# Turning normalised rows: TensorE transposes, or VectorE blocks regrouped through device memory

## The chip, the cores and the metric

The kernel runs on one core of a Trainium2 chip. The metric is the device time of one execution in microseconds (us); a profiled execution also gives a trace, whose span runs from the first to the last instruction. The engines are named as in the profile: PE is TensorE (PEld its weight loads), DVE is VectorE, ACT is ScalarE, POOL is GpSimd, SP is SyncE, which issues nearly all DMA transfers here.

## The reference

The input x has 16 sequences of 256 tokens with 256 features, 4096 tokens in all, in float32. Two layers follow one another; each normalises, runs a mixer `s` and a gated network `g` on the normalised rows, and adds their product:

```python
xn = _layernorm(x, axis=-1)
s = _L0_attn_ref(xn, ...)          # linear recurrence over time, 32 complex states
g = _silu(_L0_ffn_ref(xn, ...))    # 256 -> 1024 (gelu) -> 256
x = x + s * g
xn = _layernorm(x, axis=-1)
s = _L1_attn_ref(xn, ...)          # causal attention, 16 heads, latent keys and values, rope
g = _silu(_L1_ffn_ref(xn, ...))    # base matrix plus routed low-rank part (top 2 of 8)
x = x + s * g
```

Every product with a weight matrix sums over the features. TensorE sums over partitions, so it needs the normalised rows with features on partitions, while the normalisation leaves tokens on partitions. Something has to turn each 128 x 128 block. How this is done is what changes here.

## The kernel before

The 4096 tokens are cut into 8 chunks of 512 (two sequences each). A chunk's rows `X[ch]` stay in SBUF as [128 tokens, 4 blocks, 256 features]. The normalised, turned chunk is `xnT`, [128 features, 2 halves, 512 tokens].

**Layer 0** is one loop over the chunks (from L454). Iteration `ch` does `hidden` (16 PE matmuls `ph`, for the chunk's two feature halves and eight blocks of the hidden layer, which the trace shows as 32 records of 512 columns, since it has two for each float32 matmul; then a gelu on ACT), `recur` (`pb`; then `v` on DVE, a swap of partition halves `w<-v` by two SP DMAs at L417 and L418, a POOL addition, a scan on DVE and a product that gives `g`), then for the next chunk `norm0` and `turn0`, and then two times `mix` (`pf`) and `finish0` (`py`, which reads `g`). PE's instructions are kept in the order of the program by the helper `InOrder` (L44 to L64); all of them therefore carry line L52 in the profile. The other engines' order in layer 0 is the framework's choice. `transpose_rows` (L156) makes eight PE transposes into PSUM (`tp`), and ACT and DVE copy one half each to `xnT`.

**Layer 1** keeps all five engines in program order. Before the loop, chunk 0 is prepared. The loop (L921) then runs over 64 units, one for each chunk, group of four heads and sequence: eight units per chunk, and `r` is the unit's place in its chunk. In the body of unit `i`:

- SP first fetches the turned probabilities of unit i-2 (`pT<-far`).
- `score_pack` runs three times (PE `sc`, DVE mask and maximum, ACT exponential), and POOL normalises.
- `turn` and `send` treat the probabilities of unit i-1: DVE transposes 32 x 32 blocks (`turned`), SP writes them to device memory in four DMAs (`far<-turned`), from where the fetch of the next unit reads them back in a regrouped order.
- In even units `query_move` issues eight DMAs (`qg<-qrot`), which put the rotated queries of the group that units i+2 and i+3 will use into place; and `values` multiplies the probabilities of units i-4 and i-3 with the values (PE `av`, reading `pT`).
- In odd units two, in even units one of the query products `pq` of a later group are made.
- The next chunk is prepared in between: `norm_begin` at r=0, `norm_end` at r=2, `transpose_chunk` at the end of r=2 (eight PE transposes, two ACT copies), `kv_begin` at r=4, `kv_end` at r=5, `router_chunk` at r=6, `key_chunk` at r=7. The output of the chunk before is finished (`po`) at r = 3, 4, 5 and 7.

Each engine works off its own list in order, so an instruction that waits holds back all behind it on its engine, also on SP's queue.

Of the kernel before, what the change touches and what calls it, by code (L numbers as in the profile page):

```python
# [11 lines left out]
F32 = mybir.dt.float32  # L12
# [6 lines left out]
P = 128  # L19
B, S, D = 16, 256, 256  # L20
NTOK = B * S
CH = 512
NCH = NTOK // CH
TPC = CH // P
# [16 lines left out]
def tile_two_layers(ctx: ExitStack, tc: tile.TileContext, d: dict, out: bass.AP):  # L41
    nc = tc.nc
# [96 lines left out]
    def layer_norm(pool, src, dst, tag):  # L139
# [10 lines left out]
        for j in range(TPC):  # L150
# [2 lines left out]
                ALU.subtract, ALU.mult,  # L153
            )

    def transpose_rows(psum, ptag, src, dst, tag):  # L156
        for c in range(2):
            ps = psum.tile([P, CH], F32, tag=ptag, name=f"tp_{tag}_{c}")
            for j in range(TPC):
                pe.transpose(  # L160
                    ps[:, j * P : (j + 1) * P], src[:, j, c * P : (c + 1) * P], ident
                )
            if c == 0:
                nc.scalar.copy(dst[:, c, :], ps)
            else:
                nc.vector.tensor_copy(dst[:, c, :], ps)

    def bc(ap, n):

        return ap.unsqueeze(1).to_broadcast([ap.shape[0], n, ap.shape[1]])  # L170
# [6 lines left out]
    with ExitStack() as l0:  # L177
# [3 lines left out]
        a2 = l0.enter_context(tc.tile_pool(name="a0", bufs=2))  # L181
        hpool = l0.enter_context(tc.tile_pool(name="h0", bufs=10))
        ps_mm = l0.enter_context(tc.tile_pool(name="ps_mm", bufs=4, space=PSUM))
# [4 lines left out]
        p1T = w0.tile([P, 2, FF], F32, tag="p1T", name="p1T")  # L188
# [27 lines left out]
        def norm0(ch):  # L216
            xn = a2.tile([P, TPC, D], F32, tag="xn", name=f"xn0_{ch}")
            layer_norm(sm, X[ch], xn, f"0_{ch}")
            return xn

        def turn0(ch, xn):
            xnT = a2.tile([P, 2, CH], F32, tag="xnT", name=f"xnT0_{ch}")
            transpose_rows(ps_mm, "mm", xn, xnT, f"0_{ch}")
            return xnT

        xn = norm0(0)
        xnT = turn0(0, xn)


# [23 lines left out]
        def tiny(name, n=1):  # L253
            return w0.tile([P, n], F32, tag=name, name=name)
# [38 lines left out]
        f = tiny("f")  # L293
# [12 lines left out]
        for k in range(1, 8):  # L306
            c, s = rot[:, k - 1, 0:1], rot[:, k - 1, 1:2]
# [10 lines left out]
        for k in range(8):  # L318
            n = 1 << k
            c, s = rot[:, k, 0:1], rot[:, k, 1:2]  # L320
# [17 lines left out]
        bT = w0.tile([P, 2, P], F32, tag="bT", name="bT")  # L338
# [52 lines left out]
        def hidden(ch, xnT):  # L391
            hT = []
            for fc in range(NFC):
                ph = ps_mm.tile([P, CH], F32, tag="mm", name=f"ph_{ch}_{fc}")
                for c in range(2):
                    pe.matmul(
                        ph, p1T[:, c, fc * P : (fc + 1) * P], xnT[:, c, :],
                        start=(c == 0), stop=(c == 1),
                    )
                ht = hpool.tile([P, CH], F32, tag="hT", name=f"hT_{ch}_{fc}")  # L400
                nc.scalar.activation(ht, ph, AF.Gelu, bias=b1[:, fc : fc + 1])  # L401
                hT.append(ht)
            return hT

        def recur(ch, xnT):

            pb = ps_mm.tile([P, 2, S], F32, tag="mm", name=f"pb_{ch}")
            for c in range(2):
                pe.matmul(
                    pb.rearrange("p b s -> p (b s)"), bT[:, c, :], xnT[:, c, :],  # L410
                    start=(c == 0), stop=(c == 1),
                )
            v = a2.tile([P, 2, S], F32, tag="v", name=f"v_{ch}")
            nc.vector.tensor_tensor(v, pb, bc(turn, 2), ALU.mult)

            w = a2.tile([P, 2, S], F32, tag="w", name=f"w_{ch}")
            nc.sync.dma_start(w[0:64, :, :], v[64:128, :, :])  # L417
            nc.sync.dma_start(w[64:128, :, :], v[0:64, :, :])  # L418
            nc.gpsimd.tensor_tensor(v, v, w, ALU.add)
            g = a2.tile([P, 2, S], F32, tag="g", name=f"g_{ch}")  # L420
            nc.vector.tensor_tensor_scan(
                g.rearrange("p b s -> p (b s)"), decay.rearrange("p b s -> p (b s)"),
                v.rearrange("p b s -> p (b s)"), 0.0, ALU.mult, ALU.add,
            )
            nc.vector.tensor_tensor(g, g, bc(turn, 2), ALU.mult)
            return g.rearrange("p b s -> p (b s)")
# [27 lines left out]
        for ch in range(NCH):  # L454
# [24 lines left out]
            xn, xnT = xn2, xnT2  # L479
# [3 lines left out]
    x1 = ctx.enter_context(tc.tile_pool(name="x1", bufs=2))  # L483
    qm = ctx.enter_context(tc.tile_pool(name="qm1", bufs=2))
    qr = ctx.enter_context(tc.tile_pool(name="qr1", bufs=1))
    a2 = ctx.enter_context(tc.tile_pool(name="a1", bufs=2))
    pp = ctx.enter_context(tc.tile_pool(name="p1", bufs=2))
    fix = ctx.enter_context(tc.tile_pool(name="fix1", bufs=1))
    qp = ctx.enter_context(tc.tile_pool(name="q1", bufs=2))
    dp = ctx.enter_context(tc.tile_pool(name="far1", bufs=3, space=bass.MemoryType.DRAM))  # L490

    sp = InOrder(nc.sync)
    ve = InOrder(nc.vector)
# [5 lines left out]
    def m1(name, shape):  # L499
        return ps_m1.tile(shape, F32, tag="m1", name=name)  # L500
# [4 lines left out]
    chunks = [Chunk() for _ in range(NCH)]  # L505
# [17 lines left out]

    def norm_end(ch):
        k = chunks[ch]
        k.xn = x1.tile([P, TPC, D], F32, tag="xn", name=f"xn1_{ch}", bufs=1)
        for j in range(TPC):
            ve.tensor_scalar(
                k.xn[:, j, :], X[ch][:, j, :], k.mv[:, j, 0:1], k.rs[:, j : j + 1],
                ALU.subtract, ALU.mult,  # L530
            )

    def transpose_chunk(ch):
        k = chunks[ch]
        k.xnT = x1.tile([P, 2, CH], F32, tag="xnT", name=f"xnT1_{ch}")
        for c in range(2):
            ps = m1(f"tp_1_{ch}_{c}", [P, CH])
            for j in range(TPC):
                pe.transpose(ps[:, j * P : (j + 1) * P], k.xn[:, j, c * P : (c + 1) * P], ident)
            ac.copy(k.xnT[:, c, :], ps)  # L540

    def kv_begin(ch):

# [275 lines left out]
    def send(u):  # L819

        u.far = dp.tile([4, 32, G, 3, P], F32, tag="far", name=f"far_{u.n}", bufs=3)
        for h in range(G):
            sp.dma_start(
                u.far[:, :, h, :, :].rearrange("k s z q -> s k z q"),
                u.turned[32 * h : 32 * h + 32, :, :, :],
            )
# [4 lines left out]
    def fetch(u):  # L831
        new_pT(u)
        sp.dma_start(u.pT, u.far.rearrange("k s h z q -> (k s) h z q"))
# [56 lines left out]

    norm_begin(0)
    norm_end(0)
    transpose_chunk(0)
    kv_begin(0)
    query_mm(0, 0)
    query_mul(0, 0)
# [24 lines left out]
    for i in range(LAST):  # L921
        ch, r = divmod(i, PER)
        odd = i % 2 == 1
        u, w = units[i], units[i - 1] if i else None
        here = w is not None and w.i >= LAST - 2
        n = (i + 3) // 2 if odd else (i + 2) // 2
        n = n if n < len(groups) else None
        more = ch + 1 < NCH
        last = ch - 1 if ch and r in FINISH else None

        if 2 <= i:
            fetch(units[i - 2])
        score_pack(u, 0)
        if w:
            normalise(w, (2,))
        if r == 1:
            gate_end(ch, 0)
        if r == 2:
            gate_end(ch, 1)
            if more:  # L940
                norm_end(ch + 1)
        if r == 5 and more:
            kv_end(ch + 1)
        if w:
            for z in (1, 2):
                turn_here(w, z) if here else turn(w, z)

        if r == 0:
            mid_chunk(ch)
        if r == 7 and more:  # L950
            key_chunk(ch + 1)
        if n is not None:
            query_mm(n, 0 if odd else 3)
            if not odd:
                query_lat(n, 3)
        score_pack(u, 1)

        if odd and n is not None:
            query_mm(n, 1)
            query_mul(n, 0)  # L960
        if w:
            if here:
                turn_here(w, 0)
            else:
                turn(w, 0)
                send(w)
        if not odd:
            if n is not None:
                query_move(n)
            if i >= 4:  # L970
                values(units[i - 4])
                values(units[i - 3])
        score_pack(u, 2)
        normalise(u, (0, 1))

        if odd and n is not None:
            query_mm(n, 2)
            query_mul(n, 1)
            query_rot(n)
            query_lat(n, 2)  # L980
        if r < 2:
            gate_begin(ch, r)
        if r == 0 and more:
            norm_begin(ch + 1)
        if r == 2 and more:
            transpose_chunk(ch + 1)
        if r == 4 and more:
            kv_begin(ch + 1)
        if r == 6 and more:
            router_chunk(ch + 1)  # L990
        if last is not None:
            j = FINISH.index(r)
            finish_mm(last, j, 0, NPAIR)
            finish_out(last, j)


    ch = NCH - 1
# [89 lines left out]
```

## Time and profile before

| | |
|---|---|
| median of 3 runs | 980.04 us (977.87 to 980.08) |
| profiled execution | 977.1 us, span 975.3 us |
| mean granted TensorE clock | 0.994 |
| PE busy | 935.6 us, 96% of the span |
| DVE, ACT, POOL busy | 60%, 44%, 44% |
| DMA packets, bytes | 197028, 136.04 MB |
| PE transposes `tp` | 128, median 273 ns each, overlapping |
| chunk of layer 0, chunk of layer 1 | 31.9 us, 82.0 us |

A timeline row gives the start and length in us, the engine, the source line, the operation, what it writes and reads, a shape and a count; in square brackets, where there is one, the idle time just before it on its engine and what ended it. The name of a tile is given without its buffer number. "SPq" rows are DMAs issued by SP, their length being the issue on SP and not the transfer; the tile view gives the time from issue to landing. A table of stretches gives for each engine the busy time and the number of instructions, then the granted TensorE clock, the mean busy share of the 16 DMA engines and GB/s.

### The profile page before, as it was taken

The numbers are of one execution on the slowest core, as the hardware profiler recorded it, in microseconds if no ns is written. First come the engines' busy times: TensorE is split into PE (matmuls) and PEld (weight loads), VectorE is DVE, ScalarE is ACT, GpSimd is POOL, SyncE is SP. The second block draws the span as 40 slices with busy tenths as digits, with TensorE's granted clock in tenths as the row PEclk, the third lists the DMA queues.
The fourth block names the chain that finished last, engine by engine and source line by source line (L and its number), as shares of the span: only waits on it lengthen the run. The fifth ranks groups of instructions, "written<-read, shape, count | busy, mean of one in ns | idle before, by whom it ended". The sixth has DMA issues, their size and how long they took to land.

```text
span 975.3 us, 15554 instructions
## 1 busy us (share of the span) xinstructions
PE 935.6 (96%) x4698; PEld 667.9 (68%) x4698; DVE 589.1 (60%) x1876; ACT 425.1 (44%) x1412; POOL 425.5 (44%) x749
## 2 busy tenths in 40 slices
PE   4999999999999989999999999999999999999986
PEld 2657657766666556777777777777777777777765
DVE  7923223221125968867876786786787679676651
ACT  2232232233324546544554454555456455455440
POOL 2316124213333545553655456456355544544542
PEclk9999999999999989999999999999999999999999
DMA  9622000000002577776767677678767776867850
GB/s 292 194 65 65 12 11 1 11 11 11 1 12 33 119 199 196 199 188 186 189 177 211 165 168 220 161 197 201 189 176 178 207 174 167 221 169 192 206 182 22
DMA packets 197028, 136.04 MB, mean 139 GB/s; under 512 B 142545, under 2 KB 186449, under 8 KB 196945
## 3 DMA queue, kind: packets, MB, share of 16 engines
q1 hardware_dynamic: 193712, 129.27, 50.9%
q0 software_dynamic: 1536, 4.20, 1.2%
q10 hardware_dynamic: 1696, 1.58, 0.7%
q8 instruction: 38, 0.62, 0.3%
q14 instruction: 46, 0.37, 0.1%
HBM read 63.18 MB, written 52.95 MB: 119 GB/s over the span
## 4 chain that ended last, share of the span: by engine, by line
PE 83%; DVE 6%; POOL 4%; DMA 3%; issue 2%; SPq 2%; ACT 0%; ACTq 0%; POOLq 0%; DVEq 0%
PE pq L52 20%; PE sc L52 13%; PE pf L52 10%; PE ph L52 10%; PE po L52 10%; PE av L52 8%; PE pg L52 4%; SPq L52 2%; PE pm L52 1%; POOL pr L52 1%; PE py L52 1%; PE pb L52 1%; PE pkv L52 1%; PE tp L52 1%; DVE nm L52 1%
## 5 line engine op out<-in xcount | busy, mean ns | idle before, releaser
L52 ACT ACTIVATE pr<-sc,nm 128x256 f32<-128x256 f32 (+7 forms) x512 | 189.5, 380 | 286.6 <-DVE sr L52 198.4
L52 POOL TENSOR_SCALAR pr<-pr,sr 128x256 f32<-128x256 f32 (+7 forms) x512 | 192.2, 394 | 275.6 <-DVE sr L52 272.6
L52 PEld LDWEIGHTS sc<-kT,qg 128*128 128x128 f32 x1024 | 159.7, 191 | 65.3 <-issue 39.5
L52 PE MATMUL sc<-kT,qg 128*128 128x256 f32 (+7 forms) x1024 | 176.6, 306 | 6.9 <-DMA qg<-qrot 4.2
L52 DVE STREAM_TRANSPOSE turned<-pr 128x512 f32<-128x512 f32 x186 | 123.2, 687 | 15.2 <-POOL pr L52 14.9
L52 DVE TENSOR_REDUCE nm<-sc 128x1 f32<-128x256 f32 (+7 forms) x512 | 127.6, 301 | 6.6
L52 PE MATMUL pq<-xnT,wlat 128*128 128x512 f32 x256 | 124.4, 609 | 0.0
L52 PE MATMUL pq<-xnT,wrope 128*128 128x512 f32 x256 | 120.1, 593 | 0.0
L52 PE MATMUL po<-wout,attT 128*128 128x256 f32 x512 | 115.8, 380 | 0.0
L52 PE MATMUL pf<-p2T,hT 128*128 128x256 f32 x512 | 113.0, 379 | 0.0
L52 PE MATMUL ph<-xnT,p1T 128*128 128x512 f32 x256 | 112.9, 600 | 0.0
L52 PEld LDWEIGHTS po<-wout,attT 128*128 128x128 f32 x512 | 96.4, 190 | 20.9 <-issue 6.6
L52 PEld LDWEIGHTS pf<-p2T,hT 128*128 128x128 f32 x512 | 96.7, 190 | 13.3 <-issue 0.5
L52 ACT ACTIVATION_READ_ACCUMULATOR pr<-sc,nm 128x1 f32 x512 | 103.5, 202 | 0.0
L52 PE MATMUL av<-pT,row 128*64 128x256 f32 (+1 forms) x1024 | 90.5, 329 | 0.3 <-DMA pT<-far 0.3
L52 PEld LDWEIGHTS ph<-xnT,p1T 128*128 128x128 f32 x256 | 49.1, 192 | 59.3 <-issue 57.9
L52 POOL TENSOR_TENSOR qrot<-qmul,qmul 128x512 f32<-128x512 f32 x64 | 83.0, 1318 | 14.6 <-DVE sc L52 9.9
L52 DVE TENSOR_TENSOR qmul<-pq,rot_q 128x512 f32<-128x512 f32 x128 | 80.7, 672 | 0.0
L52 PEld LDWEIGHTS av<-pT,row 128*64 128x64 f32 x1024 | 64.2, 137 | 23.1 <-PE av L52 0.5
L52 ACT ACTIVATE qg<-pq 64x512 f32<-64x512 f32 x128 | 75.4, 589 | 6.7 <-PE pq L52 6.0
L52 DVE TENSOR_TENSOR sc<-sc,kmask 128x96 f32<-128x96 f32 (+1 forms) x192 | 45.8, 238 | 51.1 <-PE sc L52 49.8
L401 ACT ACTIVATE hT<-ph,b 128x512 f32<-128x512 f32 x64 | 44.0, 687 | 59.0 <-PE ph L52 58.9
(178 smaller groups left out, 906.1 us busy)
## 6 DMA issues: line engine op xcount, KB each, us to landing
far<-turned SPq DMA_DIRECT2D x248, 192.0 KB, 3.7
pT<-far SPq DMA_DIRECT2D x62, 768.0 KB, 4.6
qg<-qrot SPq DMA_DIRECT2D x256, 64.0 KB, 2.4
out_dram<-o POOLq DMA_DIRECT2D x32, 128.0 KB, 2.9
x<-in_x_dram SPq DMA_DIRECT2D x7, 512.0 KB, 8.7
wqn<-in_wq_nopeT_dram SPq DMA_DIRECT2D x4, 512.0 KB, 4.7
wo<-in_Wo_dram SPq DMA_DIRECT2D x4, 512.0 KB, 5.3
w<-v SPq DMA_DIRECT2D x16, 128.0 KB, 2.3
```

Of the source, the lines that this page charges most:

```text
L52: r = getattr(self.engine, name)(*args, **kw)
L401: nc.scalar.activation(ht, ph, AF.Gelu, bias=b1[:, fc : fc + 1])
```

## The change

In 13 of the 16 chunk passes (chunks 2 to 7 of layer 0, chunks 1 to 7 of layer 1) the rows are no longer turned on PE. DVE turns 32 x 32 blocks within each group of 32 partitions (`turn_rows`, two instructions per chunk); four SP DMAs, one for each group of partitions, write the blocks to a buffer in device memory; and further DMAs read it back so that the blocks lie on their partitions.

In layer 0 the fetch is one DMA with 4 KB in a row per partition. The tile `xnT` gets the order (block of partitions, half, row block, 32 tokens), and its readers `ph` and `pb` take it through the view `tokens`, in runs of 32 elements. Chunks 0 and 1 are still turned on PE, into the same order.

In layer 1 `xnT` keeps its order, and the fetch is four DMAs that each write 128-byte runs. `rows_begin` (DVE) follows `norm_end` in unit r=2, `rows_send` (SP) stands after that unit's `send` and before its `query_move`, and `rows_fetch` (SP) is the first thing in unit r=3, before the fetch of probabilities. Chunk 0 is still turned on PE. The normalised rows `xn` move to the tag `tmp`, which they share with temporaries of `kv_begin` and `router_chunk`.

```diff
+    def tokens(xnT, c):
+        return xnT[:, :, c, :, :].rearrange("p b j s -> p j b s")
...
+    def turn_rows(v, t, src):
+        for c in range(2):
+            v.transpose(
+                t[:, :, c, :, :].rearrange("p k j s -> p j k s"),
+                src[:, :, c * P : (c + 1) * P].rearrange("p j (k f) -> p j k f", f=32),
+            )
...
         def turn0(ch, xn):
-            xnT = a2.tile([P, 2, CH], F32, tag="xnT", name=f"xnT0_{ch}")
-            transpose_rows(ps_mm, "mm", xn, xnT, f"0_{ch}")
+            xnT = a2.tile([P, 4, 2, TPC, 32], F32, tag="xnT", name=f"xnT0_{ch}")
+            if ch < 2:
+                transpose_rows(ps_mm, "mm", xn, xnT, f"0_{ch}")
+                return xnT
+            t = a2.tile([P, 4, 2, TPC, 32], F32, tag="turnx", name=f"turnx0_{ch}", bufs=1)
+            far = dp0.tile([4, 32, 4, 2, TPC, 32], F32, tag="farx", name=f"farx0_{ch}")
+            turn_rows(nc.vector, t, xn)
+            for b in range(4):
+                nc.sync.dma_start(
+                    far[:, :, b, :, :, :].rearrange("k f c j s -> f k c j s"),
+                    t[32 * b : 32 * b + 32, :, :, :, :],
+                )
+            nc.sync.dma_start(xnT, far.rearrange("k f b c j s -> (k f) b c j s"))
             return xnT
...
                     pe.matmul(
-                        ph, p1T[:, c, fc * P : (fc + 1) * P], xnT[:, c, :],
+                        ph.rearrange("p (j b s) -> p j b s", j=TPC, b=4),
+                        p1T[:, c, fc * P : (fc + 1) * P], tokens(xnT, c),
...
-        k.xn = x1.tile([P, TPC, D], F32, tag="xn", name=f"xn1_{ch}", bufs=1)
+        k.xn = a2.tile([P, TPC, D], F32, tag="tmp", name=f"xn1_{ch}", bufs=1)
...
+    def rows_begin(ch):
+        k = chunks[ch]
+        k.turned = pp.tile([P, 4, 2, TPC, 32], F32, tag="turnx", name=f"turnx_{ch}", bufs=1)
+        turn_rows(ve, k.turned, k.xn)
+
+    def rows_send(ch):
+        k = chunks[ch]
+        k.far = dp.tile([4, 32, 4, 2 * TPC, 32], F32, tag="farx", name=f"farx_{ch}", bufs=2)
+        for b in range(4):
+            sp.dma_start(
+                k.far[:, :, b, :, :].rearrange("k f y s -> f k (y s)"),
+                k.turned[32 * b : 32 * b + 32, :, :, :, :].rearrange("f k c j s -> f k (c j s)"),
+            )
+
+    def rows_fetch(ch):
+        k = chunks[ch]
+        new_xnT(ch)
+        for b in range(4):
+            sp.dma_start(
+                k.xnT.rearrange("p c (j b s) -> p (c j) b s", b=4, s=32)[:, :, b, :],
+                k.far[:, :, b, :, :].rearrange("k f y s -> (k f) y s"),
+            )
...
+        if r == 3 and more:
+            rows_fetch(ch + 1)
         if 2 <= i:
             fetch(units[i - 2])
...
             if more:
                 norm_end(ch + 1)
+                rows_begin(ch + 1)
...
                 turn(w, 0)
                 send(w)
+            if r == 2 and more:
+                rows_send(ch + 1)
         if not odd:
             if n is not None:
                 query_move(n)
...
-        if r == 2 and more:
-            transpose_chunk(ch + 1)
```

More of the change, by code (lines that the diff above doesn't have):

```diff
@@ L162, in transpose_rows @@
                 )
+            view = ps.rearrange("p (j b s) -> p j b s", j=TPC, b=4)
             if c == 0:
-                nc.scalar.copy(dst[:, c, :], ps)
+                nc.scalar.copy(tokens(dst, c), view)
             else:
-                nc.vector.tensor_copy(dst[:, c, :], ps)
+                nc.vector.tensor_copy(tokens(dst, c), view)
+    def turn_rows(v, t, src):
[4 more added lines that the diff above has]
+            )
     def bc(ap, n):
@@ L219, in norm0 @@
             return xn
+        dp0 = l0.enter_context(tc.tile_pool(name="far0", bufs=2, space=bass.MemoryType.DRAM))
         def turn0(ch, xn):
-            xnT = a2.tile([P, 2, CH], F32, tag="xnT", name=f"xnT0_{ch}")
-            transpose_rows(ps_mm, "mm", xn, xnT, f"0_{ch}")
+            xnT = a2.tile([P, 4, 2, TPC, 32], F32, tag="xnT", name=f"xnT0_{ch}")
[11 more added lines that the diff above has]
+            nc.sync.dma_start(xnT, far.rearrange("k f b c j s -> (k f) b c j s"))
             return xnT
@@ L409, in recur @@
                 pe.matmul(
-                    pb.rearrange("p b s -> p (b s)"), bT[:, c, :], xnT[:, c, :],
+                    pb.rearrange("p i (j b s) -> p (i j) b s", j=2, b=4),
+                    bT[:, c, :], tokens(xnT, c),
                     start=(c == 0), stop=(c == 1),
@@ L531, in norm_end, with new_xnT, transpose_first @@
             )
-    def transpose_chunk(ch):
-        k = chunks[ch]
-        k.xnT = x1.tile([P, 2, CH], F32, tag="xnT", name=f"xnT1_{ch}")
+    def new_xnT(ch):
+        chunks[ch].xnT = x1.tile([P, 2, CH], F32, tag="xnT", name=f"xnT1_{ch}")
+    def transpose_first():
+        k = chunks[0]
+        new_xnT(0)
         for c in range(2):
-            ps = m1(f"tp_1_{ch}_{c}", [P, CH])
+            ps = m1(f"tp_1_{c}", [P, CH])
             for j in range(TPC):
@@ L892, in tile_two_layers @@
     norm_end(0)
-    transpose_chunk(0)
+    transpose_first()
     kv_begin(0)
```

## The prediction

> **What bounds the kernel now.** First the page's busy shares and, by stage, the table of stretches (length, then busy time of PE, PEld, DVE, ACT, POOL; granted clock; DMA share; GB/s).
>
> ```profile
> PE 935.6 (96%) x4698; PEld 667.9 (68%) x4698; DVE 589.1 (60%) x1876; ACT 425.1 (44%) x1412; POOL 425.5 (44%) x749
> ```
>
> ```profile
> 126.00:286.00 160.00, 158.97 (x585) 105.89 (x584) 37.36 (x65) 49.52 (x65) 44.83 (x35) 1.00 0.04 9
> ...
> 490.00:572.00 82.00, 82.00 (x460) 60.43 (x458) 61.57 (x196) 42.26 (x162) 42.31 (x83) 1.00 0.71 184
> ```
>
> TensorE is full in both layers: a layer-1 chunk is 82.00 us, all PE. PE work removed is time gained, if nothing that PE consumes comes later. Layer 0 leaves the DMAs idle (0.04); layer 1 has them at 0.71. Next, the timelines around the transposes of one layer-1 chunk: PE (start, length), then DVE, then SP's queue.
>
> ```profile
> 491.15 1.07 PE L52 MATMUL tp<-ident,xn 128*128 128x128 f32 x8
> 492.05 0.98 PE L52 MATMUL sc<-kT,qg 128*128 128x256 f32 x4
> ...
> 502.96 0.97 PE L52 MATMUL sc<-kT,qg 128*128 128x256 f32 x4
> ...
> 506.40 2.82 PE L52 MATMUL av<-pT,row 128*64 128x256 f32 x32
> ```
>
> ```profile
> 487.06 2.36 DVE L52 TENSOR_SCALAR xn<-x,mv,rs 128x256 f32<-128x256 f32 x4
> 489.34 1.29 DVE L52 STREAM_TRANSPOSE turned<-pr 128x512 f32<-128x512 f32 x2
> 490.56 0.23 DVE L52 TENSOR_TENSOR sc<-sc,kmask 128x96 f32<-128x96 f32 x1
> 490.82 0.79 DVE L52 TENSOR_REDUCE nm<-sc 128x1 f32<-128x192 f32 x3
> 491.53 0.70 DVE L52 STREAM_TRANSPOSE turned<-pr 128x512 f32<-128x512 f32 x1
> ```
>
> ```profile
> 492.26 2.22 SPq L52 DMA_DIRECT2D far<-turned  x4
> 494.58 6.31 SPq L52 DMA_DIRECT2D qg<-qrot  x8
> 500.94 0.62 SPq L52 DMA_DIRECT2D pT<-far  x1
> ```
>
> The reader is to see how far behind PE this is. SP's sends and query moves of unit 2 (r=2) run while PE is in unit 3. The eight qg moves feed the first score of unit 4, at 502.96. The last is issued at about 500.26 and a qg transfer lands 2.3 us after its issue, so at 502.6: 0.4 us to spare. In the five later repeats of this place the same arithmetic gives 0.1 to 1.0. The pT fetch of 500.94 lands 5.8 us later (tile view), at 506.7; its values are the second half of the 32 at 506.40, due at 507.8: spare 1.1, mean 1.4 over six chunks. So the thin margin is on SP's queue, not on PE, though it shows as no wait at all. The one place where it failed is chunk 0:
>
> ```profile
> 344.67 1.94 PE L52 MATMUL sc<-kT,qg 128*128 128x256 f32 x4 [4.24 <-DMA qg<-qrot]
> ```
>
> ```profile
> 345.00:350.00 5.00, 5.00 (x10) 2.68 (x10) 2.23 (x6) 0.99 (x4) 3.08 (x5) 0.52 0.87 288
> ```
>
> **The change, layer 1** (seven chunks).
> Removed from PE: eight transposes, 492.05 - 491.15 = 0.90 us per chunk. ACT loses two copies of 0.63 us; ACT is 52% busy, worth nothing.
> DVE gains two 128x512 block transposes before the three of this unit: 1.3 us by the row above (1.29 for two). DVE has no idle gap from 487.06 to 492.2, so all behind is 1.3 us later: the softmax of unit 2, whose score buffers PE needs again in unit 3 (released at about 492.9 for a score at 494.58, spare 1.7, less 0.9 for the earlier PE: PE loses some 0.5 there, lost anyway by what follows), and the send on SP.
> SP, sends: four DMAs put between the send and the query moves, each 128 pieces of 1 KB. Nearest row: far, 128 pieces of 1.5 KB, four in 2.22 us, 2.3 with the gap.
> So the query moves are 1.3 + 2.3 = 3.6 us later. The last lands at 502.6 + 3.6 = 506.2; PE, ready at about 502.1, starts unit 4 at 506.2 instead of 502.96. The removed 0.90 is swallowed by this wait.
> SP, fetches: four DMAs put ahead of unit 3's pT fetch, each 1024 pieces of 128 B. The trace has no such DMA. Issue lasts 0.43 us for 128 pieces (far) and 0.63 for 512 (qg), so by that slope about 0.9 for 1024, 3.9 for four with the gaps. From below: no dearer than qg, 2.5 to 2.9. From above: the transfer paces the queue, 2 us each, 8 in all. I take 3.9, as the issue rows are nearest. They read what the sends wrote, but the eight query moves (some 6 us) lie between, so I expect no wait on landing.
> So the pT fetch is 3.6 + 3.9 = 7.5 us later. Less the mean spare 1.4, PE's second half of the values is 6.1 us later than now. This wait ends last and includes the 3.2 before it. Behind it on SP, unit 3's send and unit 4's moves are late too, but the next moves, issued at 512.03, have until unit 6 (526.07, itself now later), so the delay ends there. PE is full afterwards and wins nothing back: six chunks x 6.1 = 36.6.
> Chunk 0: its qg wait has no spare, +3.6; its pT has (second half due 352.1, landing 342.94 + 5.8 = 348.7), so nothing more. Layer 1: **+40**.
> New xn storage in the tmp tag: the former user was read by mid_chunk two units before, and kv_begin comes two units later; no wait.
>
> **Two rules of the Trainium skill that speak against it.** The row: after the 4.24 us wait the granted clock was 0.52 over 345 to 350, and four score matmuls took 1.94 instead of 0.97; waits of 1.9 us in the trace did nothing. The skill ("TensorE: Matmul & The Clock Gate", HAM oscillation) puts the limit at PE gaps of about 3.4 us and half speed. My qg gap is 3.5 to 4.1 us, so this may now come in each chunk. Half speed for the 6.8 us seen costs 3.4 us, but from unit 4's start to the second values PE has only 4.85 us of work: 506.2 + 4.85 + 3.4 = 514.4, against the pT landing at 500.94 + 7.5 + 5.8 = 514.2. So by row or rule the sum moves 0.2 us; the pT wait covers it, and without that cover it is 3.4 per chunk.
> For 128-byte pieces: by the row, 512 land in 2.3 us, SBUF to SBUF. "DMA: Bandwidth & Descriptors" (Specifications, Why small descriptors are slow) asks for at least 512 B, and says that the penalty concerns HBM, which is now the source. If it doubles what a fetch takes, about 2 us each, it is the upper end above: +10 per chunk in place of 6.1. No run shows it; I keep the row, and the rule for the range.
>
> **The change, layer 0** (chunks 2 to 7).
> PE loses 0.87 us per chunk (177.72 - 176.85). The view of a chunk that has no transposes says what is then late: the state matmul.
>
> ```profile
> 208.71 1.04 PE L52 MATMUL tp<-ident,xn 128*128 128x128 f32 x8
> ...
> 280.54 1.10 PE L52 MATMUL py<-csc,g 128*128 128x256 f32 x4 [1.03 <-DVE g L425]
> ```
>
> py waits for g. In the chunk of 208.71, g ends at 215.87 and py starts at 216.49; 0.87 us earlier is 215.62, so 0.25 to 0.4 goes into waiting, and up to 1.03 by the last chunk. Chunk 2's iteration waits there already (0.59): nothing. Five x about 0.5: **-2.5**, between -5.2 and +1.
> Turning and regrouping is hidden: xn is ready at 199.7, its consumer (ph) starts at 225.1. Two DVE turns of 1.3 (less a copy of 0.69; DVE is 23% busy), four sends 2.3, landing 3.7 (far), one fetch of 128 pieces of 4 KB, 4.6 (pT): about 12 us. Should SP first wait for w<-v at 209.7, it still ends by about 222. Without cover: several us per chunk.
> ph and pb now read xnT in runs of 32 elements. No row shows that; I take zero, as the count streamed is the same; 5% of 8 x 15.4 us would be 6.
>
> **Sum.** 40 - 2.5 = +37.5 on the profiled 977.1 (span 975.3), 1014.6; that execution is 2.9 below the median 980.04, so **1017**.
>
> **Rivals.**
> (a) Only qg is late, the fetches being as cheap as qg or pT landing sooner: 3.2 x 6 + 3.6 - 2.5 = +20, 1000. For: the issue cost of 1024 pieces is extrapolated. Against: two delays, 3.6 and at least 2.5, pass a spare of 1.4.
> (b) 128-byte reads pace the queue: 10 x 6 + 3.6 - 2.5 = +61, 1041. For: the rule. Against: qg's pieces are as short and cheap.
> (c) Faster. One mechanism: the query moves' place on SP. If they come no more than the spare 0.4 to 1.0 us later, and the fetches within 1.4, all is hidden: 7 x 0.9 + 2.5 (to 5.2) = 9 to 11.5 gained, 970. It decides at 0.6 us of added SP and DVE time, where I count 3.6; chunk 0, which waits already, speaks against.
> (d) No change: gains of 9 against one late place of about 1.3 us per chunk.
>
> **How the numbers follow.** Main case 0.60 (own range 1004 to 1032), (a) 0.16, (b) 0.15, (c) 0.06, (d) 0.03. Range 992 to 1050, leaving out (c), (d) and some of the tail of (b). About 0.3% is what a measurement of this kernel can tell from no change. Faster 0.06, same 0.03, slower 0.91.
>
> **What would show it.** PE waits at each chunk's unit 4: some 3.5 us on qg, then about 3 on pT (or half clock between); layer-1 chunks of about 88 us instead of 82; tp 128 instructions down to 24; SP issues of rows: sends 0.55 each, fetches about 0.95; py waits of 0.3 to 1 us. It is wrong if SP's added issues are short, if the fetch waits for the sends' landing, or if strided reads slow ph.

## The result and the profile after

The changed kernel takes 1027.73 us (median of 6 runs, 1024.02 to 1033.85) against 980.06 us (977.87 to 981.91): a ratio of 1.0492, with a 95% interval of 1.0458 to 1.0526. Its profiled execution took 1025.91 us with a span of 1024.1 us, 48.8 us more than the 975.3 us before.

The page's busy shares of the changed kernel, and its table of stretches for the middle of layer 0 and one chunk of layer 1 (length, busy time of PE, PEld, DVE, ACT, POOL, granted clock, DMA share, GB/s):

```profile
PE 944.2 (92%) x4594; PEld 665.7 (65%) x4594; DVE 602.5 (59%) x1896; ACT 416.4 (41%) x1392; POOL 424.7 (41%) x749
```

```profile
126.00:286.00 160.00, 157.38 (x558) 103.28 (x557) 37.25 (x63) 47.20 (x61) 44.27 (x36) 1.00 0.10 28
509.00:597.00 88.00, 81.71 (x436) 59.27 (x436) 61.06 (x194) 41.41 (x160) 42.32 (x83) 0.98 0.73 182
```

PE has 104 instructions less and is no longer full: in a layer-1 chunk it is busy for 81.7 of 88.0 us, where it was busy for 82.0 of 82.0. No other engine became full; DVE has 61 us in the chunk as before. So most of the time went into waits of PE, and the timelines show which. PE's busy time over the whole run rises all the same, by 8.6 us, because some of its work runs at half speed behind such waits: the mean granted clock falls from 0.994 to 0.979. PE of the changed kernel, from unit r=3 to unit r=4 of the chunk that the prediction worked on:

```profile
511.43 1.09 PE L52 MATMUL sc<-kT,qg 128*128 128x192 f32 x6 [0.39 <-ACT pr L52]
...
523.02 1.05 PE L52 MATMUL sc<-kT,qg 128*128 128x256 f32 x4 [2.95 <-DMA qg<-qrot]
...
526.53 1.52 PE L52 MATMUL av<-pT,row 128*64 128x256 f32 x16
531.01 2.54 PE L52 MATMUL av<-pT,row 128*64 128x256 f32 x16 [2.95 <-DMA pT<-far]
```

Then DVE and SP's queue for the same place:

```profile
504.19 2.35 DVE L52 TENSOR_SCALAR xn<-x,mv,rs 128x256 f32<-128x256 f32 x4
506.58 1.30 DVE L52 STREAM_TRANSPOSE turnx<-xn 128x512 f32<-128x512 f32 x2
507.80 1.26 DVE L52 STREAM_TRANSPOSE turned<-pr 128x512 f32<-128x512 f32 x2
```

```profile
510.69 2.23 SPq L52 DMA_DIRECT2D far<-turned  x4
512.96 2.65 SPq L52 DMA_DIRECT2D farx<-turnx  x4
515.77 5.31 SPq L52 DMA_DIRECT2D qg<-qrot  x8
521.13 2.85 SPq L52 DMA_DIRECT2D xnT<-farx  x4
524.02 1.12 SPq L52 DMA_DIRECT2D pT<-far  x1
```

The reader is to see PE's two waits, first for the query moves, then for the second half of the turned probabilities, and the two new rows of SP's queue (farx, and xnT from farx) that stand ahead of what PE waits for. Laid over the chunk before at the start of its normalisation (487.06 before, 504.19 after, so 17.13 us are added to the times before):

| event | before + 17.13 | after | later by | predicted |
|---|---|---|---|---|
| SP's send of probabilities | 509.39 | 510.69 | 1.30 | 1.3 |
| first query move | 511.71 | 515.77 | 4.06 | 3.6 |
| unit 4's first score on PE | 520.09 | 523.02 | 2.93 | 3.2 |
| fetch of probabilities issued | 518.07 | 524.02 | 5.95 | 7.5 |
| second half of the values on PE | 524.93 | 531.01 | 6.08 | 6.1 |

Where all the 48.8 us lie follows from one instruction that stands once in each chunk, the first `pkv`:

- Layer 0 ends 0.5 us later (last `py` over at 289.93 instead of 289.42).
- The step from there to the first `pkv` of layer 1 takes 7.12 us instead of 2.22: +4.9.
- The seven intervals from one chunk's `pkv` to the next grow by 3.64, 8.07, 7.81, 6.15, 6.46, 5.68 and 4.78, in all +42.6.
- After the last `pkv`: +0.8.

The step between the layers, on PE before and then after, and on DVE after:

```profile
288.39 1.03 PE L52 MATMUL py<-csc,g 128*128 128x256 f32 x4
290.29 1.06 PE L52 MATMUL tp<-ident,xn 128*128 128x128 f32 x8 [0.88 <-DVE dx L450]
```

```profile
288.90 1.03 PE L52 MATMUL py<-csc,g 128*128 128x256 f32 x4
294.93 2.25 PE L52 MATMUL tp<-ident,xn 128*128 128x128 f32 x8 [5.00 <-issue]
```

```profile
294.42 1.38 DVE L52 TENSOR_SCALAR xn<-x,mv,rs 128x256 f32<-128x256 f32 x4 [3.76 <-POOL x L481]
```

Chunk 0's rows for layer 1 are now normalised only after POOL's last addition of layer 0 (L481), though they read X[0], which had been finished long before. In the kernel before they were made at 149.5 to 151.5. PE waits 5.00 us and then runs its transposes at half speed (2.25 us instead of 1.06). "issue" beside the wait means only that the profile names no releaser; DVE's row names it.

Layer 0, on PE:

```profile
83.85 1.72 PE L52 MATMUL py<-csc,g 128*128 128x256 f32 x4 [2.22 <-DVE g L454]
...
185.83 1.13 PE L52 MATMUL py<-csc,g 128*128 128x256 f32 x4 [1.20 <-DVE g L454]
```

The waits of 1.04, 0.16 and 0.21 us in the next iterations have the same form. The second `py` of an iteration lies, against before, at +2.37, +1.54, +0.72, +1.31, +1.75, +1.30, +0.51 in iterations 1 to 7. From one to the next, four of them save 0.45 to 0.83 us, but iteration 1, the first that turns on DVE, loses 2.4, and iterations 4 and 5 lose 0.6 and 0.4. The reason is in the rows of DVE around 80, of SP around 177 and of POOL there:

```profile
80.08 1.30 DVE L177 STREAM_TRANSPOSE turnx<-xn 128x512 f32<-128x512 f32 x2
...
81.76 1.22 DVE L450 TENSOR_TENSOR_SCAN g<-decay,v 128x512 f32<-128x512 f32 x1
```

```profile
177.75 0.34 SPq L250 DMA_DIRECT2D xnT<-farx  x1
178.51 0.47 SPq L446 DMA_DIRECT2D w<-v  x1
```

```profile
182.53 1.26 POOL L448 TENSOR_TENSOR v<-v,w 128x512 f32<-128x512 f32 x1 [15.43 <-DMA w<-v]
```

In iteration 1 the turn of the rows (1.30 us) stands ahead of the scan that `py` waits for, where a copy of 0.68 us stood before. That makes the first `py` only 0.7 us later than before; the other 1.7 of the 2.4 us are half clock behind the wait (granted clock 0.57 over 84 to 88): from the first `py` to the second it is 9.53 us instead of 7.87. Later the turn is early, but the fetch goes out only when `pb` has read the old rows (177.72): `xnT` has two buffers, both in use until then. So 512 KB are fetched just while the swap w<-v runs, whose landing takes a median of 3.3 us instead of 2.3, and `g` comes that much later.

### The profile page after: what moved, and what is told of

Read it like the earlier page. It is cut to its first block, busy times and chain, and to the rows that moved or that the text cites. A ratio compares the mean times of both kernels' runs of the same rounds, so it can differ in the third digit from the quotient of the medians.

```text
span 1024.1 us, 15475 instructions
## 1 busy us (share of the span) xinstructions
PE 944.2 (92%) x4594; PEld 665.7 (65%) x4594; DVE 602.5 (59%) x1896; ACT 416.4 (41%) x1392; POOL 424.7 (41%) x749
## 4 chain that ended last, share of the span: by engine, by line
PE 66%; DVE 14%; DMA 8%; SPq 4%; POOL 3%; issue 2%; ACT 2%; POOLq 0%; DVEq 0%; ACTq 0%
PE pq L52 15%; PE sc L52 10%; PE ph L52 9%; PE po L52 8%; PE pf L52 6%; PE av L52 6%; DMA pT<-far 4%; SPq L52 4%; PE pg L52 4%; DVE turned L52 2%; DVE nm L52 2%; DVE xn L52 2%; PE py L52 1%; ACT pr L52 1%; PE pkv L52 1%
## 5 line engine op out<-in xcount | busy, mean ns | idle before, releaser
L52 PE MATMUL sc<-kT,qg 128*128 128x256 f32 (+7 forms) x1024 | 179.8, 311 | 32.2 <-DMA qg<-qrot 23.0
L52 PE MATMUL pq<-xnT,wlat 128*128 128x512 f32 x256 | 129.1, 629 | 0.0
L52 PE MATMUL av<-pT,row 128*64 128x256 f32 (+1 forms) x1024 | 93.1, 332 | 9.6 <-DMA pT<-far 9.3
L52 PEld LDWEIGHTS pq<-xnT,wlat 128*128 128x128 f32 x256 | 47.9, 200 | 34.1 <-issue 33.9
```

The costliest lines, as they stand in the source:

```text
L52: r = getattr(self.engine, name)(*args, **kw)
```

## Experiments

All are timed against the kernel before on the same chip; its medians there were 978.59 to 979.11 us. Theory T is the prediction's: the rows' DMAs, by their place on SP's queue, and DVE's two turns make the query moves and then the probabilities late. Its rivals are that the transfers themselves (128-byte pieces) are the cost wherever they stand, and that the cost lies outside layer 1's loop.

**Layer 1's part alone** (layer 0 as before):

```diff
-            if ch < 2:
+            if ch < NCH:
                 transpose_rows(ps_mm, "mm", xn, xnT, f"0_{ch}")
```

> Layer 1 as changed, layer 0 turned on PE as before. By the ledger of the two traces (layer 0 +0.5 us, the step between the layers +5, layer 1 about +43): within 3 us of the changed kernel, about 1027 us. If layer 0's part gained the 2.5 us that were predicted, this kernel is 2.5 slower than the changed one, 1030; if layer 0's part costs, it is faster than the changed one by that.

1031.15 us, ratio 1.0516 (1.0489 to 1.0542). The interval overlaps that of the whole change: all of the loss is in layer 1's part.

**Layer 0's part alone** (layer 1 as before, `xn` in its own tag, PE transposes in unit r=2):

```diff
-        if r == 3 and more:
-            rows_fetch(ch + 1)
...
-                rows_begin(ch + 1)
...
-            if r == 2 and more:
-                rows_send(ch + 1)
...
+        if r == 2 and more:
+            transpose_chunk(ch + 1)
```

> Layer 0 as changed, layer 1 as before (rows turned on PE, own tag for xn). Ledger: 980.5 us, no gain, since py waits for g instead of the transposes being done. The prediction's step said -2.5: 977.5. If PE time in layer 0 were what counts, -5.2: 975.

978.06 us, ratio 0.9995 (0.9981 to 1.0009). Eight transposes less on PE in each of six chunks of layer 0 gain nothing that can be measured; the waits of 2.24, 1.14 and 1.12 us for `g` are there in this kernel too. The predicted gain of 2.5 us is not found: the interval leaves room for 1.9 at most.

**The tag of the normalised rows alone** (the kernel before with this one line):

```diff
-        k.xn = x1.tile([P, TPC, D], F32, tag="xn", name=f"xn1_{ch}", bufs=1)
+        k.xn = a2.tile([P, TPC, D], F32, tag="tmp", name=f"xn1_{ch}", bufs=1)
```

> The kernel before with nothing changed but the place of layer 1's normalised rows (tag tmp instead of an own tag). Theory: the buffer lies over memory that layer 0 uses to its end, so chunk 0's rows are normalised only after layer 0's last POOL instruction; PE waits some 5 us between the layers and then runs at half clock for a while: 985 to 987 us. The prediction's step said no wait: 980.

985.12 us, ratio 1.0069 (1.0044 to 1.0095). PE in this kernel:

```profile
295.15 2.25 PE L52 MATMUL tp<-ident,xn 128*128 128x128 f32 x8 [5.00 <-issue]
```

The same wait of 5.00 us as in the changed kernel. The first interval behind it is 0.5 us longer, and all later ones are as before (73.68, then 81.99 us). So the step between the layers is the price of the tag, once, and the loop pays nothing for it. The prediction had looked for a wait inside the loop only.

**The order on SP's queue** (sends behind the query moves, fetches behind the fetch of probabilities):

```diff
-            if r == 2 and more:
-                rows_send(ch + 1)
         if not odd:
             if n is not None:
                 query_move(n)
+            if r == 2 and more:
+                rows_send(ch + 1)
...
-        if r == 3 and more:
-            rows_fetch(ch + 1)
         if 2 <= i:
             fetch(units[i - 2])
+        if r == 3 and more:
+            rows_fetch(ch + 1)
```

> The changed kernel with only SP's order altered: the four sends of the rows behind unit 2's eight query moves instead of ahead, the four fetches behind unit 3's fetch of probabilities instead of ahead. Theory (place on SP's queue): the moves are late only by the 1.3 us of the two DVE turns, the probabilities by 1.3 + 2.7 less a spare of 1.4, so some 2.6 us per chunk in place of 6.2: 1003 to 1008 us. Rival (the transfers of 128-byte pieces themselves, or DVE, cost the time): no better than 1020 us.

1010.52 us, ratio 1.0314 (1.0294 to 1.0335): 17 us of the 48 come back from order alone, with the same DMAs. SP's queue and PE in this kernel:

```profile
512.88 5.80 SPq L52 DMA_DIRECT2D qg<-qrot  x8
518.73 2.07 SPq L52 DMA_DIRECT2D farx<-turnx  x4
520.84 0.46 SPq L52 DMA_DIRECT2D pT<-far  x1
521.39 5.93 SPq L52 DMA_DIRECT2D xnT<-farx  x4
```

```profile
606.20 1.05 PE L52 MATMUL sc<-kT,qg 128*128 128x256 f32 x4 [0.68 <-DVE o L52]
...
611.87 1.52 PE L52 MATMUL av<-pT,row 128*64 128x256 f32 x16 [0.64 <-DMA pT<-far]
...
615.05 2.02 PE L52 MATMUL pkv<-wkva,xnT 128*128 128x128 f32 x16 [0.87 <-DMA xnT<-farx]
```

The 3.0 us wait of unit 4 is down to 0.7, the wait for probabilities to 0.6; in their place `pkv` waits for the rows themselves (in two of the seven chunks the profile names ACT, but the last row had landed only 0.07 us earlier). Behind the fetch of probabilities the four fetches take 5.93 us on SP instead of 2.85, 3.46 of it the third alone. The time is 2.5 us above the expected 1003 to 1008; the wait of `pkv`, 0.7 to 1.9 us in each of seven chunks, would be more than enough for that. With DVE's two turns and all transfers still in unit 2 and 3, chunks are 84.6 to 86.2 us, not 82.

**The rows' DMAs issued by ACT** in place of SP:

```diff
     def rows_send(ch):
-            sp.dma_start(
+            ac.dma_start(
...
     def rows_fetch(ch):
-            sp.dma_start(
+            ac.dma_start(
```

> The changed kernel, but the four sends and four fetches of the rows in layer 1 are issued by ACT instead of SP; the same DMA engines move the same pieces. Place on SP's queue: the moves are late by the DVE turns alone (1.3 us), the probabilities within their spare, so 1 to 2 us per chunk in place of 6.2, less what ACT's own eight issues (some 5 us per chunk, in an engine 52% busy) delay: 992 to 1005. Transfers of 128-byte pieces as the cause: the probabilities still land late, 1015 or more.

1032.23 us, ratio 1.0539 (1.0514 to 1.0564), far outside what the theory of the queue's order expected. SP's queue in this kernel, while ACT issues the rows' eight DMAs between 517.7 and 525.4:

```profile
518.13 4.30 SPq L52 DMA_DIRECT2D far<-turned  x4
523.37 7.32 SPq L52 DMA_DIRECT2D qg<-qrot  x8
```

SP's four sends take 4.30 us instead of 2.23, and its eight moves 7.32 instead of 5.31: 4.1 us more on SP, which is more than the 2.8 us that the rows' sends had taken there themselves. The wait for probabilities is gone, the waits for the moves grow to between 2.9 and 4.6 us (7.25 in chunk 0). What SP itself waited for between 517 and 531 (in all, times, longest):

```profile
SPq L52 <- DMA farx<-turnx: 3.4, 2, 2.6
SPq L52 <- DMA xnT<-farx: 2.1, 3, 0.9
```

These are the rows' DMAs that ACT had issued, and nothing that SP sends or moves reads their data. The trace's semaphore records show the tie: the DMAs of both queues take turns at eight completion semaphores, and an issue waits until the DMA that last had its semaphore has landed. SP's third move goes out at 525.47, when ACT's first fetch, issued at 520.76, has landed at 525.45; the fourth at 526.98 follows ACT's second fetch, which landed at 526.97. In the changed kernel, with one queue, the semaphores of this stretch were free when their turn came. So SP's two rows are longer by waiting, 2.6 us within the sends and 2.1 within the moves, and not by dearer issues. The run does not speak against the theory of SP's queue: in this program a DMA on ACT still holds up SP's moves, and now until it has landed. Besides, ACT issues in the midst of its exponentials, and PE waits 0.8 to 1.8 us per chunk for `pr`.

**A better place for the rows' work** (layer 0 on PE): normalised and turned in unit r=1, sent after that unit's send, fetched in unit r=3 behind the probabilities, chunk 0's `xn` in the buffer `turnx`:

```diff
+            if more:                      # r == 1, after gate_end
+                norm_end(ch + 1)
+                rows_begin(ch + 1)
...
-            if r == 2 and more:
+            if r == 1 and more:
                 rows_send(ch + 1)
```

> Layer 0 turned on PE as before; in layer 1 the rows are normalised and turned in unit r=1 (which has no query moves), sent in r=1 behind that unit's send, fetched in r=3 behind the fetch of probabilities, chunk 0's rows in the buffer of the turned blocks. If place in the queues is the whole cost, the 0.9 us of PE per chunk comes free: 974 to 976, at most 6.3 us faster. If DVE's 3.7 us in unit 1 make the scores late, or the fetch comes too late for kv_begin, 980 to 990.

992.09 us, ratio 1.0141 (1.0118 to 1.0164). Chunks are down to 82.5 to 82.8 us, but waits of 1.1 to 1.4 us for the moves remain: DVE now runs without a gap from 404 to 422, statistics, normalisation, turns and gate in one, and the send of unit 2 goes out at 421.46, right behind the last of these turns. The step between the layers is still there (5.01 us).

**The same with layer 0 on DVE and three buffers for xnT there**:

```diff
-            xnT = a2.tile([P, 4, 2, TPC, 32], F32, tag="xnT", name=f"xnT0_{ch}")
+            xnT = a2.tile([P, 4, 2, TPC, 32], F32, tag="xnT", name=f"xnT0_{ch}", bufs=3)
```

> The same, with layer 0 as changed but three buffers for the turned rows instead of two, so that its fetch need not wait for the state product and does not run beside the swap of v. If the swap's delay is what takes layer 0's gain, 2 to 3 us faster than the kernel without it; if the chain to g sets it anyway, no difference.

986.95 us, ratio 1.0074 (1.0052 to 1.0096), 5 us less than with layer 0 on PE. The later `py` of layer 0 now wait 0.15 to 0.21 us and the iterations take 31.42 us instead of 31.86 (185.76 to 217.18). That confirms the cause found in the trace: with the third buffer the fetch goes out 4.9 us ahead of the swap (174.56 and 179.50), not 0.8, and no longer meets it. Iteration 1 still waits 2.23 us behind the turn, so that in the profiled executions layer 0 gains only 1.0 us; the rest is spread over layer 1 and the end, and its cause was not followed up.

**Chunk 0's rows in turnx** (the changed kernel, with only this):

```diff
+        if ch == 0:
+            k.xn = pp.tile([P, TPC, D], F32, tag="turnx", name=f"xn1_{ch}", bufs=1)
```

> The changed kernel, but chunk 0's normalised rows of layer 1 lie in the buffer of the turned blocks (unused by chunk 0) instead of the tag tmp. If tmp's place is what holds the step between the layers, 4 to 6 us less than the changed kernel: 1022 to 1024. If that buffer too lies over memory that layer 0 still uses, or if the wait has another cause, no difference: 1028.

1031.24 us, ratio 1.0532 (1.0503 to 1.056), and the step shows the same 5.01 us and the same releaser as above: this buffer too becomes free only when layer 0 ends. It gained nothing.

**Chunk 0's rows in xnT's second buffer** (the changed kernel, with only this):

```diff
+        if ch == 0:
+            k.xn = x1.tile([P, TPC, D], F32, tag="xnT", name=f"xn1_{ch}")
```

> The changed kernel, but chunk 0's normalised rows of layer 1 lie in the second buffer of xnT, which stands where xn stood before. The buffer of the turned blocks brought nothing, with the same wait on layer 0's last POOL addition. If any memory that layer 0 holds to its end makes the wait, and this place is free early, PE's 5.0 us between the layers go and the half clock after it: 5 to 6 us less, 1022. If the wait comes from something else than the place, 1028.

1024.70 us, ratio 1.0459 (1.0431 to 1.0488). PE:

```profile
293.92 1.06 PE L52 MATMUL tp<-ident,xn 128*128 128x128 f32 x8 [0.88 <-DVE dx L479]
```

The wait is 0.88 us again and the transposes run at full speed, so the step is as before. The time is about 3 us less than the changed kernel's, though the two intervals overlap, so that the gain itself is not secured.

**All corrections in layer 1** (layer 0 on PE): statistics already in unit r=5 of the chunk before, normalisation and turns at the end of r=0, send in r=1, fetch in r=3 behind the probabilities, chunk 0's rows in xnT's buffer:

```diff
-        if r == 0 and more:
-            norm_begin(ch + 1)
+        if r == 0 and more:
+            norm_end(ch + 1)
+            rows_begin(ch + 1)
+        if r == 5 and ch + 2 < NCH:
+            norm_begin(ch + 2)
```

> As placed, but the rows are normalised and turned at the end of unit r=0, where DVE waits for PE (statistics moved to r=5 of the chunk before), so that DVE is not late in units 1 and 2, and chunk 0's rows lie in xnT's second buffer. Theory: what remained in placed was DVE's 1.3 us of turns in a stretch without DVE idle time (query moves 1.0 to 1.4 us late) and the step between the layers; without both, chunks of 81.1 us, no step: 973 to 975. If DVE is late again, or the query moves are late for another reason, 978 to 985.

976.53 us, ratio 0.998 (0.9968 to 0.9993): level with the kernel before, within 0.3%. From the third chunk on every interval is 81.16 us, 0.83 less than before and without a wait of PE: the saving that the change was made of, kept. In the second chunk a wait of 4.09 us, which the profile puts down to DVE's statistics (the last query move had landed only 0.25 us before they ended), and one of 1.37 on the moves take most of it back.

**The same, and layer 0's chunks 4 to 7 on DVE** with three buffers (chunks 0 to 3 on PE, so that no turn meets iteration 1):

```diff
-            if ch < 2:
+            if ch < 4:
                 transpose_rows(ps_mm, "mm", xn, xnT, f"0_{ch}")
```

> placed2, with layer 0's chunks 4 to 7 turned by DVE too and three buffers for the turned rows (chunks 0 to 3 on PE, since DVE's turns stood ahead of the scan in the second iteration). With three buffers the state product was late by only 0.15 us, so 4 x 0.45 = 1.8 us less than placed2: 971 to 974. If layer 0 holds no gain, the same as placed2.

971.08 us (970.78 to 972.77), ratio 0.9923 (0.9901 to 0.9945): faster than both kernels. That is 5.5 us less than the previous experiment, where 1.8 were expected. Of the 9.3 us between the two profiled executions 3.3 lie in layer 0; 5.2 lie in the second chunk, whose wait of 4.09 us with half clock behind it is one of 1.86 at full speed here, for a reason that was not followed up. Its chunk in the table of stretches, PE at unit r=4, and SP:

```profile
488.00:570.00 82.00, 82.00 (x459) 60.26 (x455) 63.59 (x197) 42.61 (x165) 42.50 (x83) 1.00 0.79 206
```

```profile
499.97 0.97 PE L52 MATMUL sc<-kT,qg 128*128 128x256 f32 x4
...
503.41 2.82 PE L52 MATMUL av<-pT,row 128*64 128x256 f32 x32
...
506.85 2.03 PE L52 MATMUL pkv<-wkva,xnT 128*128 128x128 f32 x16
```

```profile
482.48 3.62 SPq L52 DMA_DIRECT2D farx<-turnx  x4
...
491.34 5.54 SPq L52 DMA_DIRECT2D qg<-qrot  x8
496.93 0.62 SPq L52 DMA_DIRECT2D pT<-far  x1
497.59 4.56 SPq L52 DMA_DIRECT2D xnT<-farx  x4
```

PE is full, in 81.16 us per chunk, with the very same turns and transfers (DMA share 0.79) that cost 6 us a chunk where the change had put them. The send is over 5 us before the moves begin, and the four fetches stand behind the fetch of probabilities and land 3.5 to 5.6 us after their issue, with no reader waiting. So neither the 128-byte pieces nor DVE's turns are a cost in themselves here. Fetching layer 1's rows in longer pieces was not tried.

## Why the prediction was right, and where its steps were not

**The place and the chain: right.** The forecast was 1017, the result 1027.7, inside the main case's own range of 1004 to 1032. The four later marks of the table come at 4.06, 2.93, 5.95 and 6.08 us where 3.6, 3.2, 7.5 and 6.1 were predicted; the last five intervals grow by a mean of 6.18. Chunk 0: +3.64 for a predicted 3.6; from its normalisation to unit 4's first score it takes 18.89 us instead of 15.35. There DVE's turns also make PE wait 3.33 us for the softmax in unit 3 (at 342.56), where the prediction reckoned with 0.5, but the later wait for the moves covers it. The waits named (queries, then probabilities, at unit 4 of each chunk) are those of the trace, and the last two experiments, which only give layer 1's work other places, take them away from the third chunk on.

**Issue costs: two wrong sizes that cancel.** The sends took 2.8 us of the queue (512.96 to 515.77), not 2.3. The fetches took 2.9 (521.13 to 524.02), not 3.9: 1024 pieces cost 0.6 to 0.9 us each, 0.7 in the mean, so the slope from 128 to 512 pieces was the wrong row to extend. The moves behind the sends took 5.31 us instead of 6.31. By issue alone the probabilities would be 1.5 us less late than predicted. But their fetch then landed in 5.6 to 6.85 us instead of 5.8 (6.85 in the chunk of the table), with the fetch of rows ahead of it on DMA engines that are all busy, where the kernel before has a DMA share of 0.79 (500 to 507):

```profile
523.00:531.00 8.00, 5.03 (x30) 3.42 (x31) 3.99 (x11) 3.77 (x13) 4.70 (x7) 1.00 1.02 233
```

That the probabilities come 6.1 us late as predicted is therefore in part luck. The slower landing fits part of what rival (b) said, as a slower neighbour and not as a slow queue; no run shows it apart from the rest. The rows landed in a median of 3.6 us. The Trainium skill ("DMA: Bandwidth & Descriptors", Why small descriptors are slow) names a penalty for small pieces in HBM, but the doubling at the prediction's upper end was its own supposition; it would have put the fetches at 8 us on the queue, and 2.9 were measured. In other surroundings the same four took 4.56 and 5.93 us, so the number belongs to this place.

**Half clock: right that it is covered, with one exception.** The table of stretches of the changed kernel after the queries' wait in three chunks (the granted clock is the third number from the end):

```profile
523.00:528.00 5.00, 4.98 (x30) 3.40 (x30) 3.28 (x10) 2.24 (x7) 4.64 (x7) 1.00 1.06 169
528.00:541.00 13.00, 10.05 (x61) 8.81 (x60) 3.37 (x13) 3.49 (x15) 4.02 (x9) 0.87 0.76 240
612.50:618.00 5.50, 5.12 (x14) 3.18 (x14) 2.23 (x6) 1.60 (x6) 4.68 (x7) 0.69 1.01 157
...
877.00:882.00 5.00, 4.91 (x30) 3.40 (x30) 3.28 (x10) 2.17 (x7) 4.57 (x7) 1.00 1.01 179
```

0.69 over 5.5 us is 3.4 us at half speed (0.31 x 5.5 / 0.5), a loss of 1.7 us, half of the 3.4 lost that the prediction reckoned with. In four of the six chunks it follows the queries' wait of 3.00 to 3.20 us, in two (waits of 2.95 and 2.98) it does not. Where it comes there, the wait for probabilities shrinks: the second values start 7.4 to 8.0 us after unit 4 with it (620.75 - 612.88 = 7.87), and 7.99 without it in the chunk of 523 (531.01 - 523.02); only the chunk of 877 has 6.74, and it has the smallest growth, 4.78. In the chunk of 523 it came after the second wait, with nothing behind it to cover it, and that interval grew by 7.81 instead of 6. The Trainium skill ("TensorE: Matmul & The Clock Gate", HAM oscillation) puts the limit at gaps of about 3.4 us; here 3.0 are enough in some chunks, and 2.22 were in layer 0's iteration 1.

**"New xn storage in the tmp tag: no wait": wrong.** This is the step that failed. The argument held for the loop, and the experiment on the tag shows no wait there. It left out chunk 0, whose rows were made during layer 0; in the new storage they wait for layer 0's last addition. +4.9 us on the trace, 6.0 in the experiment, once.

**Layer 0, -2.5: wrong by 3.0.** The waits of `py` were expected at 0.3 to 1 us and the DMAs hidden. The fetch was assumed to start when the sends had landed. It waits for `pb` to release the buffer, and so meets the swap; and iteration 1 had no room for DVE's 1.3 us. Reading `xnT` in runs of 32 elements costs nothing: an iteration's 32 records of `ph` take 13.90 us and its `pb` 1.88, before and after.

**The sum.** Predicted +37.5; step between the layers +4.9, layer 0 +3.0, layer 1 +42.6 instead of +40 (the uncovered half clock, and a further wait of 1.72 us in the second chunk), end +0.8: 48.8. Rival (a) had the issue cost right, since a fetch of rows is about as cheap as a move, but the probabilities do wait, and so it is out. The mechanism of rival (c) is real: the last kernel keeps the moves from being late and is 7.5 us faster than the kernel before. Between the profiled executions it is 6.3 us, 1.7 in layer 0 and 4.6 behind it, where rival (c) counted 2.5 (to 5.2) and 6.3.

## What to carry to other kernels

Before adding a DMA to an ordered queue, work out for every transfer behind it when it lands and when its reader is due: here a spare of 0.4 to 1.4 us that no wait showed decided over 40 us. The same DMAs cost nothing once they stood where both the queue and the engine that feeds them had idle time, so look for the place first and give up the change second. Before moving DMAs to another engine's queue, look at what the first queue's issues wait for: with completion semaphores shared by both, the delay stays. When a buffer moves to a shared tag, ask of its very first user, too, whose memory it takes over.

## What the runs showed of the hardware that was not expected

- A second queue did not free the first. With eight DMAs moved from SP to ACT, SP's four sends went from 2.23 to 4.30 us and its eight moves from 5.31 to 7.32 us. The cause lies in the program and not in the queues: SP waited 5.5 us for ACT's DMAs to land, because both take turns at the same eight completion semaphores. The Trainium skill ("DMA: Bandwidth & Descriptors", Rules for kernel authors) says that spreading DMAs over engines brings no bandwidth and only saves issue time; here it saved none.
- The same four fetches of 1024 pieces took 2.85, 4.56 and 5.93 us to issue. Ahead of the fetch of probabilities none of them took over 0.9 us; in the kernels that issue them right behind it, the third alone takes 2.35 to 3.7 us in every chunk, whether the sends were just before or 11 us earlier. What holds it was not taken apart.
- Half clock for 3.4 us came after PE waits of 3.0 us, in some chunks and not in others with nearly the same wait, and once after one of 2.22.
